# Preparing weight maps during the image load and fetching them later from DRAM

## The chip, the cores and the metric

The kernel runs on one core of one Trainium2 chip, in one launch. Its time is the device time of that launch in microseconds (us). The engines are named as in the profile: PE (TensorE, matrix products), PEld (its weight loads), DVE (VectorE), ACT (ScalarE), POOL (GpSimd) and SP (SyncE). A small q after a name is that engine's instruction queue where it issues transfers (SPq, ACTq).

## The reference

Four images x of 128 channels and 64 x 64 positions (float32) go through four layers. Shortened to what matters here, with t the image as 128-wide tokens:

```python
x = x + L0_conv(group_norm(x))          # deformable 3x3 convolution, 8 groups, gathers, batch norm, silu
x = L1_conv(x)                          # two Mamba-2 scans, then o = batch_norm(...); x = sigmoid(o @ conv4_w + conv4_b) * x + x
t = to_tokens(x)                        # 16,384 tokens of 128
t = t + L2_attn(layer_norm(t))          # cumprod(cos(.)) per head, layer_norm, then relu(q @ w1.T + b1) @ w2.T (2048 hidden), layer_norm
t = t + L2_ffn(layer_norm(t))           # mixture of 8 experts, best 2 of softmax(t @ router_w + router_b)
t = t + L3_attn(layer_norm(t))          # scores_ij = sum_a w2_a tanh(f_ia + g_ja + b1_a) + b2, causal, no softmax shift
t = t + L3_ffn(layer_norm(t))           # as L2_ffn with weights of its own
```

In the mixtures, `expert_out = einsum("bnd,edc->bnec", x, expert_w) + expert_b`. The kernel takes x as normalised with its last (128th) channel replaced by 1, which needs changed weights: from each of the 128 rows of expert_w (128 x 1024) and router_w (128 x 8) the last row is subtracted, and then the last row is replaced by the bias. Below this is called preparing the experts' maps. In the attention the same trick and a split of the 16 terms into two sets give the maps hide, wf, wg, cw, sb, sw (128 x 644 numbers together).

## The kernel before, in words

The image X (128 x 16,384 float32, 8 MB) stays in SBUF for the whole program. The stages run one after another. By the profile's times they are: layer 0 up to some 870 us; layer 1 up to 1689; layer 2 with the gates up to 2398; the first mixture `moe(2)` up to 2719; the attention up to some 4660; the second mixture `moe(3)` to the end.

**Order of the work.** Instructions that are issued through an `InOrder` object (line 83, which is why most lines of the profile carry that number) stay in the order in which the program writes them. All others (here called plain) are placed by a scheduler among them. Each engine executes its own queue strictly in order, and so does each queue of transfers. SP and ACT issue transfers; their transfers share eight semaphores in turn, so that a ninth is issued only when the transfer eight places before it has landed.

**Start (layer 0).** SP loads the image as eight transfers of 1 MB (line 163), ACT loads the columns, rows and weights (lines 100, 101, 119) and then fills the edges of four tables in DRAM with zeros, 16 transfers `tab<-zero` (lines 248 and 250). DVE forms the statistics of the first image (`st`, `mv`), PE sums them over groups (`pg`), DVE forms rstd (line 278), ACT takes its root (line 279), and DVE scales the weights with it (`wn`, line 297). Only then do the products `psp` begin.

**Gates (first part of layer 2).** The end of layer 1 is x times (1 + sigmoid(conv4_w @ o)). The 32 pieces of o (128 x 512) lie in DRAM; `gate(k)` loads one as `oin` (line 1565, four buffers), multiplies it on PE (`psg`), takes the sigmoid on ACT and multiplies X on DVE, and two gates later turns the piece into tokens on PE. Four gates run first, and the others are written between the steps of the first groups of layer 2, according to

```python
GATES, LAST_GATES = (0, 1, 1, 1, 2, 2, 2, 2), (0, 1, 1, 1, 2, 2, 1, 0)
for p in range(-3, NG + 1):
    for s in range(8):
        slot(p, s)
        for _ in range(GATES[s] if p < -1 else LAST_GATES[s] if p < 0 else 0):
            gate(next(steps))
```

`slot(p, s)` holds the eighth part of one group's feed-forward, and beside it steps of the groups around it: for group p + 3 its first statistics (stA, meanA) and norm, for p + 2 the products on POOL (`a_products`, ending in `u`) and second statistics (stB, meanB), for p - 1 the last sum and norm (x, stD, meanD, then u and X). Before the gates, 16 small transfers of 8 rows each fill `w1s` (line 1530), from which DVE makes the feed-forward's first map in four operations (lines 1537 to 1540), with a 0/1 column `half` from POOL's iota.

**Seam between layer 2 and the first mixture.** `attention_maps` (line 2066 on) makes the attention's maps with some 55 small operations on DVE, small products on PE (`aux`) and an iota `pi` and an affine select on POOL. `moe_prepare` (line 1815 on) makes the experts' maps: two products of 512 columns (`pse`, line 1842), a subtraction over 128 x 1024 (line 1844), the bias rows by SP (lines 1848 and 1849), and four copies of the router's map into `rws` (line 1852).

**Seam between the first mixture and the attention.** `moe_prepare` runs again for layer 3, the attention stores X to DRAM as `kept` (line 2169, four transfers of 2 MB), POOL fills a column of the tiles `v` (line 2220), and the first statistics follow: bn_stats on DVE, `variance` on POOL in seven operations, the root on ACT, `v` on DVE.

Of the kernel before, what the change touches and what calls it, by code (L numbers as in the profile page):

```python
# [17 lines left out]
P = 128  # L18
# [71 lines left out]
class Kernel:  # L90
# [33 lines left out]
    def layer0(self):  # L124
# [19 lines left out]
        with ExitStack() as outer:  # L144
            fp = outer.enter_context(tc.tile_pool(name="d0x", bufs=1))
            over = fp.tile([1, 1], I32, name="over")
            with ExitStack() as ctx:
# [17 lines left out]
                w_out = self.load(cp, "w_out", [P, P])  # L165

# [1332 lines left out]
    def layer2(self):  # L1499
# [8 lines left out]
        with ExitStack() as ctx:  # L1508
# [19 lines left out]
            for k in range(NK):  # L1528
                for r in range(4):
                    nc.sync.dma_start(w1a[32 * k + 8 * r:32 * k + 8 * r + 8], w1v[:, :, k, :])  # L1530
            half = cp.tile([P, 1], I32, name="half")
            parts = cp.tile([P, 2], F32, name="parts")
            nc.gpsimd.iota(half, pattern=[[0, 1]], base=0, channel_multiplier=1)
            nc.vector.tensor_scalar(half, half, 4, 1, ALU.arith_shift_right, ALU.bitwise_and)
            nc.vector.tensor_copy(parts[:, 1:2], half)
            nc.vector.tensor_scalar(parts[:, 0:1], parts[:, 1:2], -1.0, 1.0, ALU.mult, ALU.add)
            nc.vector.tensor_copy(w1b.bitcast(F32R), w1a)
            nc.vector.tensor_sub(w1a, w1a, w1b)
            nc.vector.tensor_scalar(w1b, w1b, parts[:, 0:1], None, ALU.mult)
            nc.vector.scalar_tensor_tensor(w1T, w1a, parts[:, 1:2], w1b, ALU.mult, ALU.add)  # L1540
            q8s = [cp.tile([P, GT, NK, 32], F32, name=f"q8_{i}") for i in range(2)]
            w2T = self.load(cp, "ffn_w2T", [P, NFC, P], eng=nc.sync)
# [5 lines left out]
            V, S, G = nc.vector, nc.scalar, nc.gpsimd  # L1548

# [9 lines left out]
            NK_ = len(kept)  # L1559

            def gate(k):
                if k < NK_:
                    ks = slice(k * 512, (k + 1) * 512)
                    o = gp.tile([P, 512], F32, name="oin", bufs=4)
                    plain.sync.dma_start(o, kept[k])
                    ps = ph.tile([P, 512], F32, name="psg", tag="phh")
                    nc.tensor.matmul(ps, conv4_w, o, start=True, stop=True)
                    x = gp.tile([P, 512], F32, name="g")
                    S.activation(x, ps, AF.Sigmoid, bias=gate_b)
                    V.scalar_tensor_tensor(self.X[:, ks], x, 1.0, self.X[:, ks], ALU.add, ALU.mult)  # L1570
# [239 lines left out]
            for _ in range(4):  # L1810
                gate(next(steps))
            for p in range(-3, NG + 1):
                for s in range(8):
                    slot(p, s)
                    for _ in range(GATES[s] if p < -1 else LAST_GATES[s] if p < 0 else 0):
                        gate(next(steps))

    def moe_load(self, ctx, layer):  # L1820
        cp = ctx.enter_context(self.tc.tile_pool(name=f"m{layer}w", bufs=1, side="right" if layer == 2 else None))
        rw = self.load(cp, f"router_w{layer}", [P, NE], eng=self.nc.sync)
        ew = self.load(cp, f"expert_w{layer}", [P, NE * P], eng=self.nc.sync)
        self.moe_maps[layer] = rw, ew

    def moe_prepare(self, ctx, layer):


        tc, nc = self.tc, self.nc
        LAST = P - 1  # L1830
        rw, ew = self.moe_maps[layer]

        cp = ctx.enter_context(tc.tile_pool(name=f"m{layer}r", bufs=1))
        rws = cp.tile([P, 4, P], F32, name="rws")
        self.moe_maps[layer] = ew, rws
        with tc.tile_pool(name=f"m{layer}i", bufs=1) as ip, \
                tc.tile_pool(name=f"m{layer}j", bufs=1, space=PSUM) as pp:
            last = ip.tile([P, P], F32, name="last")
            nc.vector.tensor_copy(last, self.ident[:, LAST:P].to_broadcast([P, P]))
            ps = pp.tile([P, NE * P], F32, name="pse")  # L1840
            for h in range(2):
                nc.tensor.matmul(ps[:, 512 * h:512 * (h + 1)], last, ew[:, 512 * h:512 * (h + 1)],
                                 start=True, stop=True)
            nc.vector.tensor_sub(ew, ew, ps)
            ps = pp.tile([P, NE], F32, name="psw")
            nc.tensor.matmul(ps, last, rw, start=True, stop=True)
            nc.vector.tensor_sub(rw, rw, ps)
            nc.sync.dma_start(ew[LAST:P, :], self.ins[f"expert_b{layer}"].rearrange("e c -> (e c)").unsqueeze(0))
            nc.sync.dma_start(rw[LAST:P, :], self.ins["rows"][ROW[f"router_b{layer}"]].unsqueeze(0))
            nc.vector.memset(rws, 0.0)  # L1850
            for j in range(4):
                nc.vector.tensor_copy(rws[:, j, 32 * j:32 * j + NE], rw)
# [211 lines left out]
    def attention_maps(self, ctx):  # L2064


        tc, nc = self.tc, self.nc
        LAST = P - 1
        cp = ctx.enter_context(tc.tile_pool(name="r3k", bufs=1))
        with tc.tile_pool(name="r3a", bufs=2, space=PSUM) as aux, tc.tile_pool(name="r3w", bufs=1) as wp:  # L2070
            w1f = self.load(wp, "att_w1f", [P, P])
            w1g = self.load(wp, "att_w1g", [P, P], view=self.ins["att_w1g"][:, 0, :])
            w2z = self.load(wp, "att_w2z", [P, 56])
            hide = cp.tile([P, P], F32, name="hide")
            nc.gpsimd.memset(hide, 0.0)
            nc.gpsimd.affine_select(out=hide, in_=hide, compare_op=ALU.is_gt, fill=1.0e4, base=0,
                                    pattern=[[1, P]], channel_multiplier=-1)
            wf = [cp.tile([P, P], F32, name=f"wf{b}") for b in range(2)]
            wg = [cp.tile([P, P], F32, name=f"wg{b}") for b in range(2)]
            cw = [cp.tile([P, 1], F32, name=f"cw{b}") for b in range(2)]  # L2080
            sb = cp.tile([P, 1], F32, name="sb")
            sw = cp.tile([P, 1], F32, name="sw")

            with tc.tile_pool(name="r3m", bufs=1) as mp:

                pi = mp.tile([P, 5], I32, name="pi")
                bits = mp.tile([P, 6], F32, name="bits")
                nc.gpsimd.iota(pi, pattern=[[0, 5]], base=0, channel_multiplier=1)
                for k in range(5):
                    nc.vector.tensor_scalar(pi[:, k:k + 1], pi[:, k:k + 1], k, 1,  # L2090
                                            ALU.arith_shift_right, ALU.bitwise_and)
                nc.vector.tensor_copy(bits[:, 0:5], pi)
                has = mp.tile([P, 2, 2, 16], F32, name="has")
                nc.vector.memset(has, 0.0)
                for b in range(2):
                    nc.vector.memset(bits[:, 5:6], float(b))
                    for hs, a0, a1 in ATT_SETS:
                        nc.vector.tensor_copy(has[hs, b, 0, a0:a1], bits[hs, 0:a1 - a0])
# [538 lines left out]
def tile_conv_attn_hybrid(ctx: ExitStack, tc: tile.TileContext, ins: dict, out: bass.AP):  # L2637
# [10 lines left out]
    with two:  # L2648
        k.moe_prepare(two, 2)
        k.moe(2)  # L2650
# [82 lines left out]
```

## Time and profile before

| | |
|---|---|
| median of 3 runs | 5025.81 us (5020.5 to 5026.61) |
| profiled execution | 5013.91 us, span 5012.2 us |
| mean granted TensorE clock | 0.942 |
| busy share of the span | PE 90%, PEld 49%, DVE 73%, ACT 72%, POOL 59% |
| transfers | 63,205 packets, 185.57 MB, mean 37 GB/s |
| start, 0 to 26 us | DMA share 0.86, 298 GB/s; DVE busy 9.46 us |
| gates, 1705 to 1747 us | PE busy 29.23, DVE 26.20, ACT 30.40, POOL 9.36 of 42 us |
| first seam, 2380 to 2401 us | PE busy 11.20, DVE 10.81, ACT 6.46, POOL 8.68 of 21 us |
| second seam, 2718 to 2731 us | PE busy 0.33, DVE 2.67, ACT 0.51, POOL 2.69 of 13 us |

A line of the timeline gives the start of an instruction or a run of like ones in us from the span's start, its busy time, the engine, the line of the program, the operation, what it writes <- what it reads by the program's names, the shapes, and the count. In brackets stands how long the engine had been idle, and what released it. A DMA view tells the packets of a stretch by size: "under 2 KB" includes those under 512 B.

### The profile page before, as it was taken

The numbers are of one execution on the slowest core, as the hardware profiler recorded it, in microseconds if no ns is written. First come the engines' busy times: TensorE is split into PE (matmuls) and PEld (weight loads), VectorE is DVE, ScalarE is ACT, GpSimd is POOL, SyncE is SP. The second block draws the span as 40 slices with busy tenths as digits, with TensorE's granted clock in tenths as the row PEclk, the third lists the DMA queues.
The fourth block names the chain that finished last, engine by engine and source line by source line (L and its number), as shares of the span: only waits on it lengthen the run. The fifth ranks groups of instructions, "written<-read, shape, count | busy, mean of one in ns | idle before, by whom it ended". The sixth has DMA issues, their size and how long they took to land. (4 is left out here: it accounts for less than half of the span.)

```text
span 5012.2 us, 65641 instructions
## 1 busy us (share of the span) xinstructions
PE 4506.2 (90%) x22570; PEld 2453.6 (49%) x22570; DVE 3670.8 (73%) x7224; ACT 3600.1 (72%) x5472; POOL 2952.8 (59%) x2907
## 2 busy tenths in 40 slices
PE   6788877788889689999797999999999999999798
PEld 4676766365667334444343444444444444444344
DVE  5999999689877488884775666766666666665675
ACT  4455453456555477776574999999999999999575
POOL 0121122255546245653487888888888878887488
PEclk9999999888779799999899999999999999999899
DMA  6665654000000200000000000000000000000000
GB/s 202 164 171 158 184 158 123 7 1 18 9 9 18 86 14 1 1 1 2 5 34 34 1 1 1 1 1 1 1 1 1 1 1 1 1 1 1 7 28 34
DMA packets 63205, 185.57 MB, mean 37 GB/s; under 512 B 10566, under 2 KB 13830, under 8 KB 61192
## 3 DMA queue, kind: packets, MB, share of 16 engines
q1 hardware_dynamic: 56856, 164.94, 11.4%
q0 software_dynamic: 2240, 12.85, 0.8%
q8 instruction: 182, 2.98, 0.2%
q10 hardware_dynamic: 3760, 3.43, 0.2%
q14 instruction: 167, 1.37, 0.1%
HBM read 131.83 MB, written 49.36 MB: 36 GB/s over the span
## 5 line engine op out<-in xcount | busy, mean ns | idle before, releaser
L83 POOL TENSOR_TENSOR r<-r 128x512 f32<-128x512 f32 (+1 forms) x1088 | 1349.8, 1242 | 331.1 <-DVE r L83 271.0
L83 DVE TENSOR_TENSOR r<-r,num 128x1024 f32<-128x1024 f32 (+1 forms) x1088 | 975.0, 927 | 598.4 <-PE num L83 495.9
L83 PE MATMUL D<-F,G 32*128 32x512 f32 (+3 forms) x4608 | 1139.1, 573 | 2.1 <-DVE den L83 0.9
L83 PE MATMUL num<-F,G 32*128 32x512 f32 (+3 forms) x4608 | 1057.4, 590 | 6.8 <-DVE r L83 3.9
L83 ACT ACTIVATE r<-r 128x2048 f32<-128x2048 f32 (+4 forms) x610 | 1018.6, 1680 | 51.0 <-POOL r L83 4.7
L83 ACT ACTIVATE r<-D 128x1536 f32<-128x1536 f32 (+1 forms) x544 | 763.5, 1404 | 49.3 <-PE D L83 29.1
L83 PEld LDWEIGHTS D<-F,G 32*128 32x128 f32 x4608 | 484.1, 184 | 373.2 <-issue 234.3
L83 PE MATMUL acc<-r,v 128*128 128x512 f32 (+3 forms) x1152 | 598.1, 606 | 0.7 <-ACT r L83 0.7
L83 PE MATMUL acc<-ident,pr 128*128 128x128 f32 x3200 | 416.6, 290 | 132.3 <-DVE pr L83 132.3
L83 POOL TENSOR_TENSOR x<-x 128x512 f32<-128x512 f32 (+2 forms) x320 | 405.8, 1268 | 153.2 <-DVE x L83 88.5
L83 PEld LDWEIGHTS num<-F,G 32*128 32x128 f32 x4608 | 383.2, 183 | 223.4 <-issue 111.1
L83 PE MATMUL pff<-hid,w_ffn_w2T 128*128 128x512 f32 x1024 | 468.6, 600 | 0.0
L83 DVE TENSOR_TENSOR pr<-v,wt 128x2560 f32<-128x2560 f32 x160 | 466.3, 2929 | 0.1
L83 PEld LDWEIGHTS acc<-ident,pr 128*128 128x128 f32 x3200 | 384.4, 150 | 167.1 <-DVE pr L83 155.9
L83 PE MATMUL pex<-w_expert_w,vT 128*128 128x512 f32 x1024 | 464.1, 601 | 1.6 <-DVE x L83 1.6
L83 PEld LDWEIGHTS acc<-r,v 128*128 128x128 f32 x1152 | 174.1, 188 | 382.7 <-issue 186.5
L83 ACT ACTIVATE x<-pex,gate 128x128 f32<-128x128 f32 x896 | 257.5, 368 | 103.8 <-PE pex L83 76.2
L83 ACT ACTIVATE hid<-phh,cols 128x512 f32<-128x512 f32 x416 | 253.1, 689 | 67.9 <-PE phh L83 67.9
L83 PEld LDWEIGHTS pex<-w_expert_w,vT 128*128 128x128 f32 x1024 | 191.9, 194 | 218.8 <-issue 163.3
L83 POOL TENSOR_TENSOR X<-X,sl 128x512 f32<-128x512 f32 x32 | 90.1, 2816 | 353.9 <-ACT sl L83 353.9
L83 POOL DMA_INDIRECT px<-tab,idx x28 | 67.0, 2394 | 367.3 <-PE pe L83 223.7
L83 PEld LDWEIGHTS pff<-hid,w_ffn_w2T 128*128 128x128 f32 x1024 | 185.0, 191 | 200.9 <-issue 200.9
(500 smaller groups left out, 7631.8 us busy)
## 6 DMA issues: line engine op xcount, KB each, us to landing
v<-tab SPq DMA_DIRECT2D x320, 256.0 KB
oms<-omw SPq DMA_DIRECT2D x32, 432.0 KB
omr<-oms SPq DMA_DIRECT2D x32, 432.0 KB
X<-in_x_dram SPq DMA_DIRECT2D x8, 1024.0 KB
tab<-vb SPq DMA_DIRECT2D x64, 128.0 KB
o<-o SPq DMA_DIRECT2D x32, 256.0 KB
oin<-o SPq DMA_DIRECT2D x32, 256.0 KB
kept<-X SPq DMA_DIRECT2D x4, 2048.0 KB
```

Source lines behind the costliest of these rows:

```text
L83: return lambda *args, **kwargs: self.tc.keep_in_program_order(op(*args, **kwargs))
```

## The change

1. `prepare_maps`, called in layer 0 behind the load of w_out, makes the attention's maps and both experts' maps in scratch tiles while the image loads, and stores them to five tiles in DRAM (`spilled`). ACT issues its loads and stores. `attention_maps`, `moe_load` and `moe_prepare` are gone.
2. `attention_space` and `moe_space` reserve SBUF for the maps before layer 2. `attention_fetch` (one load of 128 x 644) and `moe_fetch` (per layer: 127 rows of expert_w's map, its bias row, and four times 127 rows of router_w's map and its bias row) are written behind the slots of p = 0, as plain transfers of SP.
3. The gates' loads come ahead: `gate_fetch` loads `oin` for the first four gates before `w1s`, and for gate k + 4 in gate k. The four DVE operations on `w1s` and the making of `half` become `first_map`, a generator whose parts run behind the slots of p = -2.
4. In the attention, `v`'s column is filled on DVE instead of POOL, `tiny` is made there, and the first two `variance` calls (those of `statistics`) run on DVE instead of POOL.

On the queues the scheduler makes of it: on ACT the loads of att_w1f, w1g, w2z, expert_w2, router_w2, expert_w3 and router_w3 stand behind w_out and ahead of w_value, w_off and the zero-fills; the five stores stand between the zero-fills. On SP the order is att's load (before the last pieces of o are stored), w2T, oin 0 to 3, the 16 of w1s, oin 4 to 7, expert_w2 (127 x 1024), its bias row, oin 8, oin 9, then router_w2's eight small loads among oin 10 to 13, expert_w3 (127 x 1024), oin 14, its bias row, oin 15 and on, with router_w3's eight among oin 18 to 21.

```diff
                 w_out = self.load(cp, "w_out", [P, P])
+                self.prepare_maps(lambda: qp.tile([P, W, TG * P], F32, name="pr").rearrange("p u c -> p (u c)"),
+                                  lambda: pt.tile([P, TG * P], F32, name="pm", tag="pt"))
...
-            for k in range(NK):
-                for r in range(4):
-                    nc.sync.dma_start(w1a[32 * k + 8 * r:32 * k + 8 * r + 8], w1v[:, :, k, :])
...
+            def first_map():
+                G.iota(half, pattern=[[0, 1]], base=0, channel_multiplier=1)
+                V.tensor_scalar(half, half, 4, 1, ALU.arith_shift_right, ALU.bitwise_and)
+                V.tensor_copy(parts[:, 1:2], half)
+                V.tensor_scalar(parts[:, 0:1], parts[:, 1:2], -1.0, 1.0, ALU.mult, ALU.add)
+                yield
+                V.tensor_copy(w1b.bitcast(F32R), w1a)
+                V.tensor_sub(w1a, w1a, w1b)
+                yield
+                V.tensor_scalar(w1b, w1b, parts[:, 0:1], None, ALU.mult)
+                V.scalar_tensor_tensor(w1T, w1a, parts[:, 1:2], w1b, ALU.mult, ALU.add)
+                yield
...
+            def gate_fetch(k):
+                fetched.append(gp.tile([P, 512], F32, name="oin", bufs=4))
+                plain.sync.dma_start(fetched[-1], kept[k])
+
+            for k in range(4):
+                gate_fetch(k)
+            for k in range(NK):
+                for r in range(4):
+                    plain.sync.dma_start(w1a[32 * k + 8 * r:32 * k + 8 * r + 8], w1v[:, :, k, :])
+            plain.sync.dma_start(w2T, self.ins["ffn_w2T"])
...
-                    o = gp.tile([P, 512], F32, name="oin", bufs=4)
-                    plain.sync.dma_start(o, kept[k])
+                    o = fetched.pop(0)
...
+                    if k + 4 < NK_:
+                        gate_fetch(k + 4)
...
+                    if p == -2:
+                        next(begun, None)
+                if p == 0:
+                    for layer in (2, 3):
+                        self.moe_fetch(layer)
+                    self.attention_fetch()
...
+    def moe_fetch(self, layer):
+        nc, LAST = self.nc, P - 1
+        ew, rws = self.moe_maps[layer]
+        nc.sync.dma_start(ew[0:LAST], self.spilled[f"ew{layer}"][0:LAST])
+        nc.sync.dma_start(ew[LAST:P], self.ins[f"expert_b{layer}"].rearrange("e c -> (e c)").unsqueeze(0))
+        for j in range(4):
+            js = slice(32 * j, 32 * j + NE)
+            nc.sync.dma_start(rws[0:LAST, j, js], self.spilled[f"rw{layer}"][0:LAST])
+            nc.sync.dma_start(rws[LAST:P, j, js], self.ins["rows"][ROW[f"router_b{layer}"]].unsqueeze(0))
...
+    def attention_fetch(self):
+        self.nc.sync.dma_start(self.att_maps, self.spilled["att"])
+
+    def prepare_maps(self, scratch, bank):
...
+        nc.scalar.dma_start(self.spilled["att"], t[:, 0:n])
+
+        _, e = cut((("ew2", NE * P), ("ew3", NE * P), ("rw2", NE), ("rw3", NE), ("last", P)))
+        for layer in (2, 3):
+            nc.scalar.dma_start(e[f"ew{layer}"], ins[f"expert_w{layer}"])
+            nc.scalar.dma_start(e[f"rw{layer}"], ins[f"router_w{layer}"])
+        nc.vector.tensor_copy(e["last"], self.ident[:, LAST:P].to_broadcast([P, P]))
+        for layer in (2, 3):
+            for name, lo, hi in (("ew", 0, 512), ("ew", 512, 1024), ("rw", 0, NE)):
+                w, ps = e[f"{name}{layer}"][:, lo:hi], bank()[:, 0:hi - lo]
+                nc.tensor.matmul(ps, e["last"], w, start=True, stop=True)
+                nc.vector.tensor_sub(w, w, ps)
+            for name in ("ew", "rw"):
+                nc.scalar.dma_start(self.spilled[f"{name}{layer}"], e[f"{name}{layer}"])
...
-                    nc.gpsimd.memset(v[:, :, LAST:P], 1.0)
+                    nc.vector.memset(v[:, :, LAST:P], 1.0)
...
-                    variance(n, q)
+                    variance(n, q, nc.vector)
```

## Prediction, made before the changed kernel was run

> **What bounds the kernel now.** I read the span's 40 slices first: PE is at 90% and the large loops of layer 0, layer 2 and the attention are full. The edits leave the order of all engines inside those loops alone, so I went to four places where engines stand idle: the start, the gates, and the two seams around the first mixture of experts. The chain of waits covers only the last tenth of the span and says nothing here. A measurement of this kernel tells about 0.2% (10 us) from no change.
>
> The timeline of the start, columns start, duration, engine, instruction, and in brackets the idle time before it with its releaser:
>
> ```profile
> 1.73 0.45 ACTq L119 DMA_DIRECT2D w_w_out<-in_w_out_dram  x1
> 14.15 0.33 ACTq L248 DMA_DIRECT2D tab<-zero  x1
> 22.59 0.15 DVE L278 TENSOR_TENSOR rstd<-gmv,pg 128x1 f32<-128x1 f32 x1 [0.68 <-PE pg L276]
> 25.18 0.68 ACTq L250 DMA_DIRECT2D tab<-zero  x1
> 25.90 0.29 ACT L279 ACTIVATE rstd<-rstd,eps 128x1 f32<-128x1 f32 x1 [17.84 <-DMA tab<-zero]
> 26.69 0.39 DVE L297 TENSOR_SCALAR wn<-w,rstd 128x344 f32<-128x344 f32 x1
> ```
>
> DVE has the statistics ready at 22.75, but ACT takes the root only after it has issued its last zero-fill of the tables. Those issues wait for older transfers: SP's and ACT's transfers share a ring of eight semaphores, so the ninth waits until the first has landed (14.15 waits for w_out, issued at 1.73: 12.4 us under a DMA busy at 0.86 and 298 GB/s by the windows view, 0 to 26 us). From ACT's rstd on, everything in layer 0 is a chain of work: DVE is busy 32.2 of the 34 us from 91 to 125, with 16.1 of 41 before that, so a late rstd is a late layer 0, one for one.
>
> The timeline of the gates, then three answers of the DMA view (12, 4 and 8 us long):
>
> ```profile
> 1689.72 11.56 SPq L1530 DMA_DIRECT2D w1s<-in_ffn_w1T_dram  x16
> 1701.32 32.03 SPq L1565 DMA_DIRECT2D oin<-o  x21
> 1704.63 5.10 PE L83 MATMUL psg<-oin,w_conv_w 128*128 128x512 f32 x6 [18.73 <-DVE w1s L1539]
> 1718.49 1.12 PE L83 MATMUL psg<-oin,w_conv_w 128*128 128x512 f32 x2 [0.82 <-ACT g L83]
> 1728.43 1.02 PE L83 MATMUL psg<-oin,w_conv_w 128*128 128x512 f32 x2
> 1741.31 0.88 DVE L83 BATCH_NORM_STATS2 stB<-u 128x6 f32<-128x128 f32 x4 [4.23 <-POOL u L83]
> ```
>
> ```profile
> DMA packets 601, 0.25 MB, mean 21 GB/s; under 512 B 120, under 2 KB 600, under 8 KB 600
> ```
>
> ```profile
> DMA packets 4, 0.00 MB, mean 1 GB/s; under 512 B 3, under 2 KB 3, under 8 KB 4
> ```
>
> ```profile
> DMA packets 148, 2.10 MB, mean 263 GB/s; under 512 B 19, under 2 KB 19, under 8 KB 20
> q1 hardware_dynamic: 148, 2.10, 62.3%
> ```
>
> Gate 0 (1704.63) waits until 16 small loads have been issued; 1718.49 is gate 8, 1728.43 gate 14. Every transfer ends with one small packet per DMA engine used. The first answer holds 15 loads of 8 rows: 480 data packets and 120 closing ones, so 8 engines each. The second holds two loads of one row: one closing packet each. The third holds kept's 128 rows with 16 closing packets, plus two one-row loads. Engines used: 16 for 128 rows, 8 for 8, 1 for 1, always in equal shares.
>
> The two seams:
>
> ```profile
> 2381.85 0.40 DVE L2090 TENSOR_SCALAR pi<-pi 128x1 int32<-128x1 int32 x5 [2.61 <-POOL pi L2088]
> 2382.99 0.69 DVE L83 TENSOR_TENSOR x<-x,ptt 128x512 f32<-128x512 f32 x1
> 2400.26 0.39 DVE L1852 COPY rws<-w_router_w 128x8 f32<-128x8 f32 x4 [1.45 <-DMA w_router_w<-in_rows_dram]
> 2400.63 1.64 DVE L83 BATCH_NORM_STATS2 w<-X 128x6 f32<-128x128 f32 x5
> 2718.33 0.72 POOL L83 TENSOR_TENSOR X<-X,x 128x256 f32<-128x256 f32 x1
> 2719.85 0.26 SPq L1849 DMA_DIRECT2D w_router_w<-in_rows_dram  x1
> 2725.71 0.39 DVE L1852 COPY rws<-w_router_w 128x8 f32<-128x8 f32 x4 [13.31 <-DMA w_router_w<-in_rows_dram]
> 2726.01 1.64 DVE L83 BATCH_NORM_STATS2 st<-X 128x6 f32<-128x128 f32 x8
> 2729.62 0.30 ACT L83 ACTIVATE rstd<-rstd,eps 128x8 f32<-128x8 f32 x1 [20.36 <-POOL rstd L83]
> ```
>
> In the first, small map operations stand in DVE's queue ahead of the last feed-forward sums. In the second, 32 bytes of router bias queue behind kept's 2 MB store, and DVE waits 13.31 us for them.
>
> **Part 1, the start: +11 us (+6 to +15).** ACT's queue gets seven more loads ahead of w_value, and five stores; 1.21 MB in and 1.39 MB out. At the 298 GB/s of this stage 2.60 MB are 8.7 us of DMA. The same by the chain: expert_w3's load waits for w_out like the zero-fill at 14.15; transfers of this stage need 8 to 12 us to land, so it is there at 22 to 27; two products (pse took 3.78 us for a pair of halves when it waited for data, 1.96 when it did not) and half of a 1.22-us subtraction each bring 25 to 30; the store lands some 4 to 7 us later as the image is through by then; one of ACT's last zero-fills waits for it, and rstd is behind. That gives 32 to 41 against 25.90; I take 37. The 55 small DVE operations (about 0.15 us each, 8 us) lie in DVE's idle time of this window (9.5 of 26 us busy); without that cover they cost at most 8 us, the end of +15. POOL's three operations fall after 4.3 us, where it idles.
>
> **Part 2, the gates: +21 us (−5 to +28).** In SP's new order come oin 0 to 3, the 16 w1s, oin 4 to 7, then expert_w2's rows as a load of 127x1024, oin 8 and 9, small router loads between oin 9 and 13, expert_w3's 127x1024, and oin 14 and on. Gate 0 goes from 1704.63 to about 1693, gate 4 from 1711.31 to about 1706 (its load is behind w1s' issues, 11.56 us): −5.4.
>
> The price of the 127-row loads is not in the trace. 127 is prime, so equal shares mean one engine, or 127. Packet price: kept's 128 packets of 16 KB took 62.3% of 16 x 8 us, 0.62 us each, so 0.156 per 4 KB; expert_w's load at 2393 gives at most 0.22 (28 us of packets over some 129 large ones). On one engine 127 of them are 20 to 28 us; on sixteen 1.3 to 1.8. The row next by count is the 128-row store (16 engines), the row next in kind is equal shares; I take one engine at 21 us, and keep both ends.
>
> expert_w2 is issued at about 1706 and is through at 1727. oin 8 has packets on every engine behind it, so gate 8 goes from 1718.5 to 1727 or later. The four 127x8 loads (32-byte packets) add perhaps 1 us each. expert_w3 follows oin 13, whose slot comes free with gate 9: issued about 1731, through at 1752. Gate 14 moves from 1728.43 to 1752.5, +24. What stands behind a late gate: its sigmoid on ACT, its product on DVE, the transposes on PE, all in written order, so everything waits. Given back: the 4.23 us that DVE waits for POOL's u at 1741.31, as POOL's chain starts before gate 14 and can catch up, less the late half-iota behind it: +21. With sixteen engines the same steps give about 0: −5.4 at the gates, and then first_map's half, queued on POOL behind u and on DVE ahead of the second statistics, gives about 5 back (2.4 us of cast, subtraction and two products, and a wait until 1741).
>
> [...] No run so far shows a 127-row transfer.
>
> **Part 3, first seam: −6.7 us (−5.5 to −8).** The feed-forward's last sum no longer stands behind pi: 2382.99 becomes 2380.2 (after its transposes of 2379.45), 2.8 earlier; the interleaved small operations (8 of 0.15 us up to ACT's rstd, and three before u) give 1.1 and 1.0 more; the rest is the wait for the bias and the copies from POOL's last X sum (2398.53) to 2400.63, of which about 0.5 stays, since the rank copy waits for POOL's iota behind that sum: 1.6 to 1.8. What is late next is POOL, whose three operations (4.08 and 2.35 us) stay.
>
> **Part 4, second seam: −6.6 us (−4 to −8).** The statistics wait for POOL's last X sum alone: 2726.01 becomes about 2719.2, −6.8. Variance on DVE: seven operations at 0.17 against POOL's 2727.80 to 2729.62, −0.8. A second set on DVE stands ahead of the vT copy of 2741.16: +1.0. The eight memsets of v and tiny move to where DVE idles.
>
> **Sum:** +11 +21 −6.7 −6.6 = +18.7. The profiled execution takes 5013.91 us (span 5012.2), 12 below the median 5025.81; on it 5032.6, on the median 5044.5. I predict 5044.
>
> **Rivals.** First, not slower: the 127-row loads are spread over many engines. Then part 2 is 0 and the sum −2.3: 5023.5, or 5008 with the lower ends. For it: 128 rows got 16. It decides when oin 8 lands before gate 7 is done, so with fewer than some 10 us for expert_w2. Second, slower still: the small 127x8 loads cost several us each, and the half stall comes on top (+5): part 2 is +33, the time 5056. Third, the start hides: stores land quickly and rstd comes only 3 us later; with one engine that is 5036, with sixteen 5015, faster. Against it: DMA is at 0.86 there.
>
> **How the numbers follow.** One engine, parts as summed: 0.5, its own range 5034 to 5054. Second rival 0.1. Spread: 0.25, mostly within 10 us of before. Start hidden with spread loads, or other gains: 0.15. Faster 0.14, same 0.25, slower 0.61. The range drops the faster tenth and the tail of the second rival: 5014 to 5057.
>
> **What would show it.** Right: ACT's first rstd at 35 to 39; gates 8 and 14 released by oin's DMA, with two stretches of some 20 us in which one DMA engine of 16 is busy; bn_stats at the seams 6 to 7 us closer to the work before. Wrong: no wait for oin above 2 us between gates 7 and 15, or an rstd before 32.

## The result and the profile after

The changed kernel takes 5043.04 us (median of 7 runs, 5039.06 to 5056.5), the kernel before 5023.74 (median of 7). The ratio of the means is 1.0052 with an interval from 1.0036 to 1.0068, so about 26 us slower (18 to 34); the medians lie 19 apart. The profiled execution after takes 5040.44 us (span 5038.7, mean granted clock 0.943), 26.5 more than the profiled one of before.

For every profile each DVE instruction was matched with the same instruction in the profile of before. The difference of the two starts is how late the kernel is at that place; what a stage costs or gives back is the change of this lateness over the stage. "After" and "again" are two executions of the changed kernel.

| lateness against the profile before, us | after | again |
|---|---|---|
| 125 us, start behind | 13.2 | 12.9 |
| 861, end of layer 0 | 14.0 | 13.8 |
| 1683, end of layer 1 | 4.5 | 9.8 |
| 1826, gates behind | 43.2 | 46.3 |
| 2339 / 2406, around the first seam | 43.2 / 36.3 | 46.2 / 39.3 |
| 2704 / 2752, around the second seam | 34.6 / 29.6 | 39.1 / 34.5 |
| 4900, in the last mixture | 27.9 | 32.3 |

The start costs 13, the gates 38.7 (36.5 again), the seams give back 6.9 and 5.0 (4.6). These steps make about +40 (+38 again). The span is only 26.5 longer: of the 13.5 between, 9.5 lie in layer 1, whose code the change leaves as it is, and the rest in small steps of at most 2 us (1.7 in the first mixture, 1.7 from the second seam to 4900).

The start after, in the timeline (the columns are those of before):

```profile
30.54 0.33 ACTq L2169 DMA_DIRECT2D kd_ew<-pr  x1
30.68 0.15 DVE L280 TENSOR_TENSOR rstd<-gmv,pg 128x1 f32<-128x1 f32 x1 [0.47 <-PE pg L278]
...
40.88 0.45 ACTq L252 DMA_DIRECT2D tab<-zero  x1
41.38 0.29 ACT L281 ACTIVATE rstd<-rstd,eps 128x1 f32<-128x1 f32 x1 [26.12 <-DMA tab<-zero]
```

DVE has rstd ready at 30.8. The root waits until 41.38 because ACT's last zero-fill (40.88) comes only when the store of expert_w3's map, eight transfers earlier in the shared ring and issued at 30.54, has landed.

The gates after, in the timeline:

```profile
1693.98 1.74 SPq L1568 DMA_DIRECT2D oin<-o  x4
1696.92 5.20 PE L83 MATMUL psg<-oin,w_conv_w 128*128 128x512 f32 x6 [6.47 <-DMA oin<-o]
1709.32 0.28 SPq L1852 DMA_DIRECT2D w_expert_w<-kd_ew  x1
1734.24 2.04 PE L83 MATMUL psg<-oin,w_conv_w 128*128 128x512 f32 x2 [16.01 <-DMA oin<-o]
1741.17 0.25 SPq L1852 DMA_DIRECT2D w_expert_w<-kd_ew  x1
1765.24 2.04 PE L83 MATMUL psg<-oin,w_conv_w 128*128 128x512 f32 x2 [20.42 <-DMA oin<-o]
```

Gate 0 (1696.92) starts 7.7 us earlier than before, though this execution enters the gates 4.5 late. Then each load of 127 rows stops PE: gate 8 (1734.24) waits 16.01 us, gate 14 (1765.24) 20.42. From the issue of each load to the gate behind it 24.9 and 24.1 us pass.

The DMA view from 1741 to 1766, in 40 slices of 0.62 us, shows what runs meanwhile:

```profile
DMA  5741000000000003725896773000000000000000
GB/s 53 193 184 26 7 26 26 26 33 26 26 26 26 26 26 85 305 75 105 328 180 233 144 223 118 26 26 26 26 26 26 20 26 26 26 26 26 26 23 26
```

At 26 GB/s the busy share rounds to 0 in this view; by the windows view it is 0.06 from 1743 to 1749, one engine of 16, and nothing else is under way but for a burst of other loads in the middle. Each row is one packet of 4 KB. In the trace the 127 packets of the first load run one behind the other from 1712.65 to 1732.83, 0.159 us each; those of the second begin at 1742.74, 1.6 us behind its issue. Each of the two loads ends with one closing packet of 4 bytes (1732.83 and 1763.98).

The first seam after, in the timeline:

```profile
2423.37 0.69 DVE L83 TENSOR_TENSOR x<-x,ptt 128x512 f32<-128x512 f32 x1 [6.95 <-PE ptt L83]
2434.21 2.34 POOL L83 TENSOR_TENSOR X<-X,u 128x1024 f32<-128x1024 f32 x1
2436.85 2.65 DVE L83 BATCH_NORM_STATS2 w<-X 128x6 f32<-128x128 f32 x8
```

The sum x waits for PE's `ptt` alone, and the statistics begin 0.3 us behind POOL's last X sum (2434.21 + 2.34). Before they began (2400.63) 2.1 us behind it:

```profile
2396.18 2.35 POOL L83 TENSOR_TENSOR X<-X,u 128x1024 f32<-128x1024 f32 x1
```

The second seam after, in the timeline:

```profile
2752.91 0.72 POOL L83 TENSOR_TENSOR X<-X,x 128x256 f32<-128x256 f32 x1
2753.66 1.64 DVE L83 BATCH_NORM_STATS2 st<-X 128x6 f32<-128x128 f32 x8 [9.39 <-POOL X L83]
2769.95 1.91 PE L83 MATMUL D<-vT,maps 128*128 128x512 f32 x2 [4.38 <-ACT rstd L83]
2771.66 1.91 PE L83 MATMUL num<-vT,maps 128*128 128x512 f32 x2
```

The wait of 13.31 us for the router's bias is gone. The statistics begin 0.75 us after the start of POOL's last sum, against 7.68 before. But the second vT's products (D and num, a pair each) take 1.91 us a pair, after 4.38 us without a product. Before, the gap was shorter and the pairs quicker:

```profile
2741.99 1.10 PE L83 MATMUL D<-vT,wf 128*128 128x512 f32 x2 [3.21 <-DVE vT L83]
2742.92 1.02 PE L83 MATMUL num<-vT,wf 128*128 128x512 f32 x2
```

This is taken up below.

### The profile page after: what moved, and what is told of

The parts are those of the page before. It is cut to its first block, busy times and chain, and to the rows that moved or that the text cites. A ratio compares the mean times of both kernels' runs of the same rounds, so it can differ in the third digit from the quotient of the medians.

```text
span 5038.7 us, 65660 instructions
## 1 busy us (share of the span) xinstructions
PE 4493.3 (89%) x22570; PEld 2444.5 (49%) x22570; DVE 3667.0 (73%) x7237; ACT 3600.9 (71%) x5472; POOL 2941.3 (58%) x2887
## 3 DMA queue, kind: packets, MB, share of 16 engines
q10 hardware_dynamic: 5056, 5.88, 0.3%
```

## The experiments

The theory was that of the prediction: two loads of 127 rows that run on one engine hold the gates' loads behind them, and the stores hold the first root. The rivals were that something else in the gates (the small 127-row loads, or the late `half`) carries the cost, and that the start costs by the work that stands in PE's and DVE's queues, not by transfers.

### The gates

**e1: expert_w's maps in 112 and 15 rows.** Nothing but the shape of the two loads is changed.

```diff
-        nc.sync.dma_start(ew[0:LAST], self.spilled[f"ew{layer}"][0:LAST])
+        for lo, hi in ((0, 112), (112, 127)):
+            nc.sync.dma_start(ew[lo:hi], self.spilled[f"ew{layer}"][lo:hi])
```

> The two loads of 127x1024 are each cut into 112 rows and 15 rows; all else is the changed kernel. Theory A (127 rows run on one DMA engine, and the oin loads behind them in SP's queue wait for it): each expert_w is through within some 3 us of its issue, no gate waits for oin more than 2 us, no stretch of 20 us at 25 GB/s. The gates, +37.5 us between the two profiles (from +5.7 before them to +43.2 behind), come down to +3 to +10: the eight small 127x8 loads and the late half are still there. Theory B (the size of the loads, the ring of eight semaphores, or the order of fetches and slots sets it): the gates stay at +30 or more, and gates 8 and 14 still wait over 10 us each.

Measured: 5008.07 us in one run (before 5013.01, median of 13 on that chip). The gates cost +1.7 us, a little under the +3 to +10 expected. In the timeline of this kernel, gate 8 no longer waits for a transfer:

```profile
1712.40 0.90 SPq L1853 DMA_DIRECT2D w_expert_w<-kd_ew  x2
...
1722.98 1.12 PE L83 MATMUL psg<-oin,w_conv_w 128*128 128x512 f32 x2 [1.70 <-ACT g L83]
```

Its DMA view from 1712 to 1720, where expert_w2's 508 KB and pieces of o pass:

```profile
DMA packets 978, 2.02 MB, mean 253 GB/s; under 512 B 121, under 2 KB 121, under 8 KB 977
q1 hardware_dynamic: 977, 2.01, 83.8%
```

That is 253 GB/s for all that passes, where one engine alone gave 26. In the trace some sixteen of the 4 KB packets are under way at once, and the 127 rows pass between 1714.57 and 1717.1. Cutting the same bytes differently takes 37 us out of the gates.

**e2: the small router loads in 112 and 15 rows as well.**

```diff
-            nc.sync.dma_start(rws[0:LAST, j, js], self.spilled[f"rw{layer}"][0:LAST])
+            for lo, hi in ((0, 112), (112, 127)):
+                nc.sync.dma_start(rws[lo:hi, j, js], self.spilled[f"rw{layer}"][lo:hi])
```

> As e1, and the eight 127x8 loads of the router maps are cut into 112 and 15 rows as well. Theory A: the gates cost -5 to +5 us against before, and the time is 30 to 40 us below the changed kernel's less what e1 leaves: about 5005 to 5013, that is from the level of before to 0.3% under it (start +13, gates 0, seams -7 and -5). Theory C (many small transfers are dear for SP, whatever their rows): 16 instead of 8 small loads add some 0.3 us of issue each, and the gates are 3 to 6 us later than in e1.

Measured: 5010.34 us (10 runs), ratio 0.9994 (0.9982 to 1.0006): no change against before. The gates cost 0.0 us, 1.7 less than e1 and within what two executions differ by. The small loads carry nothing that can be told.

**e3: 124 and 3 rows.** A size between: if equal shares decide, 124 rows go on four engines.

```diff
-        for lo, hi in ((0, 112), (112, 127)):
+        for lo, hi in ((0, 124), (124, 127)):
```

> As e1, but cut into 124 and 3 rows. 124 is 4 x 31, so equal shares allow 4 engines, not 8 or 16. Theory A with equal shares: a plateau of some 100 GB/s, 5 to 6 us for each expert_w; gates 8 and 14 wait at most a few us, and the gates are +5 to +15. If shares need not be equal (124 rows on 16 engines): as e1, no plateau. If any number that 16 does not divide falls back to one engine: 20 us at 25 GB/s as in the changed kernel.

Measured: 5019.37 us in one run, gates +3.7 (a little under the expected +5). Timeline, then the DMA view from 1722 to 1738:

```profile
1722.05 0.69 SPq L1853 DMA_DIRECT2D w_expert_w<-kd_ew  x2
1735.12 2.05 PE L83 MATMUL psg<-oin,w_conv_w 128*128 128x512 f32 x2 [5.15 <-DMA oin<-o]
```

```profile
DMA  9999973223489339866789597222222221010100
GB/s 297 348 348 343 297 282 133 87 118 108 118 307 323 67 82 271 236 159 159 246 230 97 143 323 190 61 87 92 102 97 97 84 62 48 22 31 9 41 0 0
```

Between the full bursts the rate stands near 100 GB/s, four times the 26 of one engine, and gate 8 waits 5.15 us, a third of 16.01. In the trace the 4 KB packets run four at a time for most of this load, from 1725 to 1733. In these three runs the rate goes by the factors of the row count: 127 rows 26 GB/s, 124 rows about 100, 112 rows no plateau at all.

By their busy shares the three sizes run on one, some four and some sixteen of the 16 engines: 0.06 for 127 rows (after, 1743 to 1749), a digit of 2 in eight slices in a row here, from 61 to 102 GB/s (four engines are 0.25), and 83.8% for 112 rows with pieces of o (e1, 1712 to 1720). That agrees with equal shares, which the prediction took as its estimate from other row counts; three sizes don't show it for every count.

**e6: `half` made early.** On top of e2, POOL's iota and DVE's three operations go back to where they stood in the kernel before, ahead of the gates.

```diff
             def first_map():
-                G.iota(half, pattern=[[0, 1]], base=0, channel_multiplier=1)
-                V.tensor_scalar(half, half, 4, 1, ALU.arith_shift_right, ALU.bitwise_and)
-                V.tensor_copy(parts[:, 1:2], half)
-                V.tensor_scalar(parts[:, 0:1], parts[:, 1:2], -1.0, 1.0, ALU.mult, ALU.add)
-                yield
```

> e2 (all loads of the maps in 112 and 15 rows), and the 0/1 column half is made where the kernel before made it, by a plain iota before the gates. Theory: in e2 the gates run some 6 us ahead of before's pace until the first map, where DVE waits for POOL's iota behind u, and lose it there; with half ready early, DVE reaches the second statistics' norm 3 to 5 us sooner, so gates from +0.15 us to -3 to -5. Rival: DVE waits for POOL's u there anyway (4.23 us before), and the four map operations on DVE (2.4 us) are what stays: -1 to +1.

Measured: 5003.30 us in one run (before 5012.4, median of 12 on that chip), and the gates at −3.5 against 0.0 in e2. In the timeline of e2, DVE stands 7.53 us before POOL's iota:

```profile
1738.46 0.13 POOL L83 IOTA half<- 128x1 int32 x1
1738.62 0.15 DVE L83 TENSOR_SCALAR half<-half 128x1 int32<-128x1 int32 x1 [7.53 <-POOL half L83]
```

In that of e6, DVE waits for POOL's u instead, for less than half of it:

```profile
1745.84 0.87 DVE L83 BATCH_NORM_STATS2 stB<-u 128x6 f32<-128x128 f32 x4 [3.22 <-POOL u L83]
```

So the late `half` costs 3.5 us in this pair, and the wait for u stays. Over all profiles the gates stand at +1.7 and 0.0 with the late `half` and good loads (e1, e2), and at −1.7 to −3.5, −2.8 in the mean, in the five with the early one (e6 and those built on it): about 3.6 between the means. What the early loads of `oin` leave as a gain, net of the fetches and of the first map that now stand among the gates, is these 1.7 to 3.5 us.

### The start

**e5: the five stores behind the first statistics.** Loads and preparation stay where the change has them.

```diff
-        nc.scalar.dma_start(self.spilled["att"], t[:, 0:n])
+        stores = [(self.spilled["att"], t[:, 0:n])]
...
                 for _ in statistics(0, nc):
                     pass
+                for to, what in stores:
+                    nc.scalar.dma_start(to, what)
```

> The maps are prepared where the changed kernel prepares them, but the four stores of expert_w and router_w are written behind the first statistics, so that they stand behind ACT's first root in its queue, and no zero-fill waits for them. Theory A (the root, at 41.38 instead of 25.90, waits for the last zero-fill, and that one for expert_w3's store, 10.3 us from issue to landing): the root falls to 31 to 34, right behind DVE's rstd (30.68), and the start costs +4 to +7 instead of +13. Theory B (2.6 MB more of transfers at 300 GB/s set the end of the zero-fills): the root stays at 36 or later. What is late next would be ACT's copies of psp, behind the stores that now stand there.

Measured: 5044.37 us in one run. The gates keep their +39.1, the start falls from 13.2 to 4.6. Its timeline:

```profile
32.81 0.16 DVE L280 TENSOR_TENSOR rstd<-gmv,pg 128x1 f32<-128x1 f32 x1 [0.48 <-PE pg L278]
33.00 0.29 ACT L281 ACTIVATE rstd<-rstd,eps 128x1 f32<-128x1 f32 x1 [17.64 <-DMA tab<-zero]
```

The root comes at 33.00 instead of 41.38, right behind DVE's rstd: the bracket names a zero-fill, but what came last is DVE at 32.81. So the stores ahead of the root cost 8.6 of the 13.2 us; the 4.6 that stay are the preparation's loads and work, which this run does not tell apart. At the end of the program this shows in no time here: the gain of 8.6 at 125 us is 6.2 at 861, and at the end of layer 1 nothing of it is to be seen (6.3 against 4.5 in one execution of the changed kernel and 9.8 in the other). Layer 1's scatter, treated last, is of that size.

**e9: loads and stores of the preparation issued by POOL.** On top of e6.

```diff
-            nc.scalar.dma_start(e[f"ew{layer}"], ins[f"expert_w{layer}"])
+            nc.gpsimd.dma_start(e[f"ew{layer}"], ins[f"expert_w{layer}"])
...
-        nc.scalar.dma_start(self.spilled["att"], t[:, 0:n])
+        nc.gpsimd.dma_start(self.spilled["att"], t[:, 0:n])
```

> As e8, but the preparation written where the changed kernel has it, ahead of the first statistics. Against e8 it tells the place in the order of PE and DVE from the queue that issues. Theory: no zero-fill waits for a store, but PE's pg stands behind the map products and these behind the loads: DVE's rstd at 29 to 33, the root right behind it, start +4 to +7, as in e5.

Measured: 5012.30 us in one run. The start costs +13.9: no gain, and the expectation was wrong. In the timeline the root no longer waits for a transfer of ACT:

```profile
34.97 4.01 PE L2167 MATMUL pm<-pr 128*128 128x512 f32 x6
...
38.84 0.57 PE L278 MATMUL pg<-d,gm 128*128 128x1 f32 x2
39.47 0.15 DVE L280 TENSOR_TENSOR rstd<-gmv,pg 128x1 f32<-128x1 f32 x1
39.65 0.29 ACT L281 ACTIVATE rstd<-rstd,eps 128x1 f32<-128x1 f32 x1 [28.96 <-DVE rstd L280]
43.98 0.15 DVE L283 RECIPROCAL rstd<-rstd 128x1 f32<-128x1 f32 x1
```

A new wait has taken the place of the old. The statistics' own product `pg` stands in PE's queue behind a run of the maps' products `pm` that began at 34.97, and DVE's reciprocal comes 4.3 us after the root, behind the maps' subtractions. But this run does not tell the place in the queues from the transfers, for it has two further waits, which e6 does not have:

```profile
19.28 0.23 DVE L175 COPY w<-w_w_value 128x128 f32<-128x128 f32 x1 [6.20 <-DMA w_w_value<-in_w_value_dram]
22.01 1.00 DVE L183 COPY w<-w_w_off 128x24 f32<-128x24 f32 x9 [2.50 <-DMA w_w_off<-in_w_off_dram]
```

With POOL's loads out at once (from 12 to 26 us 388 GB/s at a DMA share of 0.99), DVE stands 8.7 us for two loads of 64 and 128 KB, and the statistics and the map work behind them come later. How much of the 13.9 is the order on PE and DVE stays open.

**e8: the same, with the preparation written behind the first statistics.**

```diff
                 w_out = self.load(cp, "w_out", [P, P])
-                self.prepare_maps(...)
...
                 for _ in statistics(0, nc):
                     pass
 
+                self.prepare_maps(...)
```

> e6, and the maps' seven loads and five stores are issued by POOL, which idles at the start, and the preparation is written behind the first statistics. ACT's zero-fills then share their semaphores with no map transfer. Theory: ACT's first root is back at 26 to 29, and what the start still costs is PE's and DVE's map work between the statistics and psp: +1 to +5 instead of +13. With gates at -3 and the seams at -7 and -5 the time is 8 to 14 us under before: ratio 0.997 to 0.9985. Rival: the 2.6 MB themselves delay the image (8.7 us at 298 GB/s): root at 33 or later, the time equal to before.

Measured: 4990.95 us (7 runs; before 5012.4), ratio 0.9954 (0.9937 to 0.9971). This is a version faster than both kernels, by 15 to 32 us against before. The start still costs 7.5, more than the theory gave it. Its timeline:

```profile
28.62 0.29 ACT L279 ACTIVATE rstd<-rstd,eps 128x1 f32<-128x1 f32 x1 [20.68 <-DMA tab<-zero]
...
34.11 0.16 DVE L281 RECIPROCAL rstd<-rstd 128x1 f32<-128x1 f32 x1
...
37.12 0.39 DVE L297 TENSOR_SCALAR wn<-w,rstd 128x344 f32<-128x344 f32 x1
```

The root comes at 28.62, only 2.7 us later than before. Then DVE's reciprocal waits 5.2 us behind small map operations, and wn 3 us more behind a subtraction that waits for PE. As the scheduler places the preparation, it goes ahead of the work that layer 0 waits for.

**e12: the preparation in pieces between layer 0's first products**, written in order as a generator, with the edit of e11 (below) as well.

```diff
-                self.prepare_maps(...)
+                preparing = self.prepare_maps(...)
+                next(preparing)
...
                         if extra is not None:
                             next(extra, None)
+                        if r < -1:
+                            next(preparing, None)
+                    if r == -2:
+                        for _ in preparing:
+                            pass
```

> All findings together: loads of the maps in 112 and 15 rows, half early, the second variance on POOL, and the preparation issued by POOL and cut into pieces that are written between the pieces of layer 0's first products (in the written order, behind the first statistics and over the first three pairs of tiles, where DVE is busy 27 of 65 us). Theory: ACT's root at 26 to 29, DVE's reciprocal right behind it (in e8 it stood 5.5 us behind map operations), start +0 to +4 instead of +7.5; gates -3.5, seams -7 and -7: 13 to 17 us under before in steps, ratio 0.9955 to 0.998 (e8: 0.9954, its layer 1 having gained as well in its profile). Rival: the pieces delay PE and DVE in the chain up to 91 us by as much as they take (some 12 us on DVE), start +8 to +12, and the time is no better than e8's.

Measured: 5007.36 us (12 runs; before 5020.12), ratio 0.9977 (0.9966 to 0.9989): faster than before by 6 to 17 us, and not shown to be better than e8 (the intervals overlap, on two chips). The start costs +8.3, the rival's figure. In the timeline the reciprocal now follows the root at once, but the root itself is late:

```profile
32.67 0.29 ACT L282 ACTIVATE rstd<-rstd,eps 128x1 f32<-128x1 f32 x1 [21.97 <-DMA tab<-zero]
33.00 0.17 DVE L284 RECIPROCAL rstd<-rstd 128x1 f32<-128x1 f32 x1 [2.89 <-ACT rstd L282]
```

So most of the cost is not the rival's: 6.8 us are the root's lateness, and only 1.4 more are lost up to 91 us, where the pieces lie. The two kernels pay in different places, and neither hides the preparation: the ring at 32.67 here, DVE's queue at 34.11 in e8.

### The second seam

**e11: the second variance back on POOL.** On top of e6.

```diff
-                    variance(n, q, nc.vector)
+                    variance(n, q, nc.vector if q == 0 else nc.gpsimd)
```

> e6, with the second set of variances in the attention back on POOL (the first stays on DVE). Prediction's step: a second set on DVE stands ahead of the vT copy and costs 1.0 us; so the second seam goes from -5 to -6. Rival: PE, at half its clock there (products of 1.9 to 2.05 us instead of 1.10), is late anyway, and moving the set back changes nothing, or loses 0.8 by the slower POOL set ahead of the root.

Measured: 4997.87 us in one run. The seam gives −7.2, against −4.3 in e6, so the one set of seven small operations on DVE costs 2.9 us, more than expected. The timeline of e6 at the second vT:

```profile
2732.59 0.68 DVE L83 COPY vT<-acc 128x512 f32<-128x512 f32 x1
...
2734.44 1.91 PE L83 MATMUL num<-vT,maps 128*128 128x512 f32 x2
```

And that of e11:

```profile
2725.68 1.10 PE L83 MATMUL D<-vT,maps 128*128 128x512 f32 x2 [3.20 <-DVE vT L83]
```

The windows view tells the granted clock behind that gap (the column after the five engines is PEclk), first of after, then of e11:

```profile
2769.90:2773.50 3.60, 3.55 (x4) 1.04 (x5) 2.79 (x9) 0.60 (x1) 0.00 (x0) 0.53 0.01 2
```

```profile
2725.60:2730.00 4.40, 4.32 (x13) 1.66 (x14) 1.75 (x7) 1.86 (x5) 1.63 (x8) 1.00 0.00 0
```

The seven operations hold vT back by 1.1 us, as PE's gap grows from 3.2 to 4.38. The clock then falls to 0.53, and the products take 1.91 us a pair instead of 1.0 to 1.1. All nine profiles with the second variance on DVE have the 4.38 and a pair of 1.91 or 1.92 behind it. Of the five with the 3.2 (the first of before, b1, b2, e11, e12) four keep the quick pairs.

At which length of a gap the clock falls, these runs don't tell. In after it is 1.00 from 2766 to 2769.9, 0.50 from 2770.1 to 2773.5, and 1.00 again from 2773.5 to 2778; in e11 it stays at 1.00 behind 3.20 us. That 3.2 us is not always safe is shown by b2 below, the fifth: it has the same gap, its clock is 0.50 from 2738 to 2746, a pair takes 2.08 us there (2740.86), and it lost 5.7 us here.

### Both kernels again

**b1 and b2: the kernel before, a1: the changed kernel, each profiled once more without an edit**, to tell what two executions of one kernel differ by.

> The kernel before, unchanged, profiled again. The steps that the two first profiles show (start +13, gates +39, seams -7 and -5) add up to +40 us, and the time rose by 26 (18 to 34); layer 1 alone gave 9.5 back between the two profiles. Theory: layer 1 of the first profile of before was a slow execution of it (granted clock 0.72 to 0.74 from 1250 to 1370 us), so here layer 1 is 5 to 15 us shorter, and the profile's other stages are the same to 2 us. Rival: the changed kernel's later start does something to layer 1, and this profile's layer 1 is as long as the first one's.

> As b1_before; two executions of the same kernel show by how much the stages scatter. Theory: layer 1 differs by up to 10 us between them, every other stage by less than 2.

> The changed kernel, unchanged, profiled again: the steps repeat (start +12 to +15, gates +37 to +40, seams -7 and -5), and layer 1 lies anywhere within 10 us.

Measured: 5020.86 and 5009.86 us for before, 5044.80 for the changed kernel. In lateness gained or lost per stage, against the first profile of before:

| us | start (125) | layer 1 (861 to 1683) | gates | first seam | second seam |
|---|---|---|---|---|---|
| b1 | −2.3 | +8.6 | 0.0 | +0.1 | 0.0 |
| b2 | −2.1 | −4.4 | −1.2 | +0.1 | +5.7 |
| after | 13.2 | −9.5 | +38.7 | −6.9 | −5.0 |
| a1 | 12.9 | −4.0 | +36.5 | −6.9 | −4.6 |
| e1 | 12.9 | −9.5 | +1.7 | −6.9 | −4.3 |
| e2 | 11.8 | −14.2 | 0.0 | −6.9 | −4.3 |
| e3 | 12.1 | −1.2 | +3.7 | −6.9 | −4.5 |
| e5 | 4.6 | −1.5 | +39.1 | −7.0 | −4.7 |
| e6 | 14.6 | −8.0 | −3.5 | −7.0 | −4.3 |
| e9 | 13.9 | −0.1 | −1.7 | −6.9 | −4.3 |
| e8 | 7.5 | −10.9 | −3.4 | −6.9 | −4.7 |
| e11 | 14.6 | −16.3 | −1.7 | −6.9 | −7.2 |
| e12 | 8.3 | −16.7 | −3.5 | −6.9 | −7.2 |

The start scatters by some 2 us, the gates by 2, the first seam by 0.1. In b2 the second seam moved by 5.7, where less than 2 was expected. Layer 1 scatters by more than 10 us in executions of one kernel and of kernels with the same code there. The theory for b1 failed: its layer 1 was 8.6 us longer, not 5 to 15 shorter. The windows view from 1250 to 1370, of the first profile of before, of b2, and of after:

```profile
1250.00:1370.00 120.00, 107.04 (x517) 73.54 (x515) 97.76 (x266) 63.45 (x120) 63.31 (x95) 0.73 0.03 9
```

```profile
1250.00:1370.00 120.00, 101.58 (x577) 68.60 (x577) 106.23 (x285) 70.17 (x132) 68.45 (x103) 0.87 0.03 10
```

```profile
1250.00:1370.00 120.00, 103.43 (x562) 70.77 (x562) 105.72 (x296) 69.22 (x129) 65.28 (x104) 0.83 0.02 7
```

The granted clock here is 0.73, 0.87 and 0.83, and in the same 120 us the trace has 517, 577 and 562 matmuls of PE. In this stretch b2 and after gain 10 and 11 us on the first profile of before. In b1 the clock is 0.73 again; its 8.6 us are lost earlier, between 950 and 1100 us. With b2, unchanged code shows both ends, so a change to the start isn't needed for it.

## Why the prediction was right, and where its steps were not

The time (5043 against 5044 predicted) and the direction were right, and the forecast's mechanism was the one that decided: e1 takes it away and the slowdown goes. That the sum agreed was luck, as two errors cancel: the steps of the change cost about +40, not +18.7, and some 14 us came back that no part of the change accounts for.

**Start, +11 forecast, +13 measured.** The mechanism (stores that hold ACT's last zero-fill and with it the root) is what e5 shows. The term that was too small is the store's landing: 4 to 7 us were taken "as the image is through by then", and it took from 30.54 to 40.88, 10.3 us. The DMA stays at 0.93 and 328 GB/s from 0 to 41 us by the windows view, and SP issues its last piece of the image only at 31.63 (24.58 before), so the image was not through. The root came at 41.4, beyond the 35 to 39 named as the sign of being right; at 125 us 13 of its 15.5 us were left, so "one for one" was nearly so. The preparation's work on DVE and PE was put down as covered by idle time. It was not quite: DVE's rstd itself came at 30.68 instead of 22.59, and with the stores out of the way (e5) 4.6 us stay, for which the map work and the loads are not told apart.

**Gates, +21 forecast, +37 to +39 measured: the step that failed.** One engine for 127 rows was right (busy share 0.06, 26 GB/s), as were gate 0 (12.2 us earlier than the end of layer 1 would put it, 11.6 forecast) and gate 4 (−5.5, forecast −5.4). Against the end of layer 1, gate 14 came 32.3 us later, not 24. The difference of 8 is made by three terms: the first load holds gate 8 for 24.9 us from its issue, where 21 were put down (3.9, less 1.2 by which it was issued earlier than 1706); expert_w3's load was issued 6.9 us behind gate 8, where 4 were taken; and it held gate 14 for 24.1 us, where 21.5 were taken. The price of the packets was right: 0.156 us each was taken and 0.159 measured, 20 and 21 us for the two times 127. What the price left out stands around them. The first packet of expert_w2 starts 3.3 us behind its issue, that of expert_w3 1.6, and from the last packet to the gate's product, with the share of o's piece that runs on the same engine, another 1.4 and 1.3 us pass. From gate 14 to the end of the gates another 6.4 us were lost, where the prediction gave 3 back: the late `half` costs about 3.6 (e6), nothing of the 4.23 came back, and the other 2.8 are not traced. In e6, with `half` early, DVE still waits 3.22 for u.

The second rival had this size (+33 for the gates, 5056), but for another reason in half of it: e1 and e2 show that its small 127-row loads cost nothing that can be told. Its other half, the half stall on top (+5), was right in kind (about 3.6). The 5008 that the first rival names for the lower ends is 5011 by the ends stated (+6, −5, −8, −8). The first rival (spread over many engines) is refuted by the plateau of 26 GB/s, the third (a hidden start) by the root at 41.38.

**First seam, −6.7 forecast, −6.9 measured**, in all eleven profiles with the change (−6.9 to −7.0). The steps hold too: x comes 2.8 us closer, as forecast, and the statistics 1.8.

**Second seam, −6.6 forecast, −4.3 to −5.0 measured.** The statistics came 6.9 us closer (forecast 6.8), the variance gave 0.8 (0.8), the second set cost 1.1 (1.0). What was missing is the consequence of that 1.1: PE's gap passes from 3.2 to 4.38 us, the products behind it run at a fallen clock (0.53), and 1.7 us more are lost. e11 takes both away and lands at −7.2.

**What stays open.** The terms measured make +40, the time shows +26 (18 to 34). In e5 steps and time agree (about +32, and 31 above the median of before, in one run). For a1 against before on its chip (5044.80 against 5002.51, 5009.86 and 5020.86) it is +35 by the middle one, and for e2 and e12 the steps' sums (about +1 and −9) lie within the intervals of their times (−9 to +3, −17 to −6). For the changed kernel in its first comparison and for e8 (sum about −7, measured −15 to −32) some 15 us are missing, and in the profiles they lie mostly in layer 1. Its mean there over the eleven changed executions is −8, over three of before +1; with a scatter of this size among three executions of before, whether layer 1 really runs shorter behind a later start is not settled.

## What to carry to other kernels

In these runs a load's row count decided its rate before its bytes did (26 GB/s with 127 rows, about 100 with 124, 253 with 112 and pieces of o): look at the factors of the first dimension, and cut 127 rows into 112 and 15, which took 37 us out of the gates here. Count what such a load holds back by the queue that it stands in, from its issue to the landing of the transfer behind it, not by its packets alone (24.9 and 24.1 us against 20 and 21). And work "prepared while something else loads" was not free here where a queue that the first critical step needs (a ring of transfers, PE's and DVE's order) had it ahead of that step; freeing one of them (e5, e8, e9, e12) showed the next each time (the start still cost +4.6, +7.5, +13.9 and +8.3 us).

## What the runs showed of the hardware

In after, one DMA engine moved 508 KB at 25 to 27 GB/s (0.159 us for each 4 KB packet) while, but for bursts of other loads, 15 stood still; 124 rows went four packets at a time at about 100 GB/s (e3), and 112 rows with pieces of o at 253 (e1). Behind a gap of 4.38 us between products the granted clock was 0.53 in after, and the products were slow in all nine profiles with that gap. One of 3.20 left it at 1.00 in e11 and the products quick in four profiles of five; in the fifth, b2, the clock fell to 0.50 and 5.7 us were lost. In layer 1 the granted clock of the same 120 us was 0.73 to 0.87 in executions of the same kernel, and the stage's length differed by 13 us (b1 against b2).
